# Eight linear-attention layers: keys from seven products of quarters, the queries' reciprocals through Ln and Exp, another elu, turned rows ahead

## The chip, the cores and the metric

The kernel runs on one core of a Trainium2 chip. The metric is the device time of one launch in microseconds; the figure for a kernel is the median over its runs. Five engines work at once, each through its own instructions in the order the program gives them: TensorE (PE, with its weight loads, PEld), VectorE (DVE), ScalarE (ACT), GpSimd (POOL) and SyncE (SP, which here only issues DMAs). All data are float32.

## The reference, cut to what matters

The input `x` is 512 rows of 512. Three blocks follow each other, each added to `x`: a cross-attention over 8192 context rows, eight layers of linear attention with a feed-forward part, and an expert block. The change touches the eight layers only. One layer is:

```
q = x @ Wq + bq;  k = x @ Wk + bk;  v = x @ Wv + bv
Q = elu(q) + 1;   K = elu(k) + 1
KV   = sum over the rows of K * v        # one number for each feature
Ksum = sum over the rows of K            # one number for each feature
Z = 1 / (Q * Ksum + 1e-6)
x = layernorm(x + gelu((Q * KV * Z) @ Wo + bo))
x = layernorm(x + gelu(gelu(x @ Wf1 + bf1) @ Wf2 + bf2))
```

There are no heads: keys, queries and values meet feature by feature, so `KV` and `Ksum` are vectors of 512.

## The kernel before, in words

The whole state stays on the chip. `curT` holds the rows of a layer turned (features on the partitions, 4 chunks of 128, 512 rows along the free dimension). A layer begins in `features`: twelve chunks of 128 output features (four of keys, four of queries, four of values), each the product of a 128-column piece of a weight with all of `curT`, summed over the four chunks of input features (`feature`, L628). Each float32 product shows as two instructions on PE.

The order on PE is written out by hand (`manual_schedule` for TensorE alone). The other engines' order is a planner's: it walks the program with estimated durations and gives each engine, at each point, the earliest emitted instruction that is ready by its estimate; `issue_after` keeps an instruction behind another in that order. Once fixed, every engine runs strictly in order.

At the start of a layer the last two of the four row tiles are not yet normalized: `finish` (L889 to L911) is still working on them, on DVE for the most part (gelu on ACT, residual, mean and variance, a root by Newton steps at L82, scaling at L906). So `features` first multiplies the 256 rows that exist for the first chunks, turns tile 2 (`turn`, L921: four transposes on PE, four copies with scale and shift on ACT at L923), goes on, turns tile 3, and makes up the second half, partly in pieces of one tile of 128 rows. Five PSUM banks of the pool `mm` hold the chunks under way, three of the pool `acc` serve the transposes and later sums.

Each finished piece goes to `taken`. Keys and queries pass `elu1`: two Relu and one Exp on ACT (L616, L618, L619), the sum with -1 on DVE (L620), and the final +1, on DVE with the running total for keys (L624), on ACT for queries (L622). A query chunk then gets `Q * Ksum + eps` on ACT (L977), its reciprocal on DVE (L978) and the product with Q on POOL (L979). A value chunk is multiplied with its keys and totalled on DVE (L983), and the total scales the query's row (L986):

```
nc.scalar.activation(y[ac], qf[ac], AF.Identity, bias=eps, scale=ksum[ac][:, 2:3])
nc.vector.reciprocal(y[ac], y[ac])
nc.gpsimd.tensor_tensor(y[ac], qf[ac], y[ac], ALU.mult)
```

The output projection (L1002) needs all four scaled chunks `vt[0]` to `vt[3]`. Then comes the first feed-forward product, in class `Seven`: two chunks (a pair `p`) at a time, features and rows cut into halves, so that a 2 by 2 product of quarters takes seven products instead of eight. POOL makes four sums of weight quarters for each pair (L710), DVE and POOL four sums of the turned rows (L716 to L719), PE does products 1 to 7 (L723) and DVE adds them up (L741, L759 to L779). The second feed-forward product (`SevenBack`, L839) does the same with the roles turned, first for row tiles 0 and 1, then (t = 2) for 2 and 3; in the latter call, tiles 0 and 1 are turned into the next layer's `curT` by `between`. After it, `affine` (L914, L915) makes the next layer's residual rows, for tiles 2 and 3 on POOL.

Weights come by DMA from SP's queue into the pool `big`: eight places of 1 MB, twelve weights a layer in the order wk, wq, wv, wo, four pieces of w1, four of w2. A load starts when its place is free; wk of the layer that starts at 1871.64 us is issued at 1789.84.

Of the kernel before, what the change touches and what calls it, by code (L numbers as in the profile page):

```python
# [16 lines left out]
P = 128  # L17
# [37 lines left out]
def perceiver_kernel(  # L55
# [513 lines left out]
    def layer_weights(l):  # L569
        w = [weights(big, m[l], f"{n}{l}") for m, n in ((wk, "wk"), (wq, "wq"), (wv, "wv"), (wo, "wo"))]  # L570
# [5 lines left out]
    first = layer_weights(0)  # L576
# [10 lines left out]
    def transpose_into(dst, src, t, space, tag):  # L587
# [4 lines left out]
        nc.scalar.copy(dst[:, :, t * P : (t + 1) * P], pt)  # L592

    with ExitStack() as s_:
# [10 lines left out]
        EARLY = 5  # L605

        eps = rpool.tile([P, 1], F32, name="eps")
        nc.vector.memset(eps, 1e-6)
        ncol = rpool.tile([P, C_BV - C_BQ], F32, name="ncol")
        nc.vector.tensor_scalar(ncol, col[:, C_BQ:C_BV], -1.0, None, ALU.mult)  # L610

        def elu1(ps, c, e, accum=None):

            n = ps.shape[-1]
            m = qkv.tile([P, n], F32, tag=f"m{n}", name="m")
            nc.scalar.activation(m, ps, AF.Relu, bias=ncol[:, c - C_BQ : c - C_BQ + 1], scale=-1.0)  # L616
            r = qkv.tile([P, n], F32, tag=f"r{n}", name="r")
            nc.scalar.activation(r, ps, AF.Relu, bias=col[:, c : c + 1])  # L618
            nc.scalar.activation(m, m, AF.Exp, scale=-1.0)  # L619
            nc.vector.scalar_tensor_tensor(m, m, -1.0, r, ALU.add, ALU.add)  # L620
            if accum is None:
                nc.scalar.activation(e, m, AF.Identity, bias=ones[:, 0:1])  # L622
            else:
                nc.vector.tensor_scalar(e, m, 1.0, None, ALU.add, ALU.add, accum_out=accum)  # L624
# [8 lines left out]
        def features(chunks, xT, turns, done):  # L633


            held = [(mm.tile([P, T], F32, tag="mm", name="ps"), *c) for c in chunks[:EARLY]]

            def tile_of(t, chunks_):
                for i in chunks_:
                    ps, w, c0 = held[i]  # L640
                    feature(ps, w, c0, xT, t * P, P)
                    if t % 2:
                        done(i, ps, (t - 1) * P, H)

            def half(t0, chunks_):
                for i in chunks_:
                    ps, w, c0 = held[i]
                    feature(ps, w, c0, xT, t0, H)
                    done(i, ps, t0, H)

            if 1 in turns:
                tile_of(0, (0, 1))
                turns[1]()
                tile_of(0, (2,))
                tile_of(1, (0, 1, 2))
            else:
                half(0, (0, 1, 2))
            half(0, (3,))
            if 1 in turns:
                turns[2]()  # L660
# [287 lines left out]
        for l in range(NL):  # L948
# [147 lines left out]
            def between(q):  # L1096
                if q in (2, 4):
                    turn(curT, gs[q // 2 - 1], q // 2 - 1, *c2)
# [276 lines left out]
```

## Time and profile before

| what | value |
|---|---|
| median of 3 runs | 2576.14 us (2575.96 to 2577.41) |
| the profiled execution: its own time | 2577.41 us |
| its span in the profile | 2575.6 us |
| PE, PEld, DVE, ACT, POOL busy, share of the span | 98%, 58%, 68%, 47%, 49% |
| the eight layers, from the first key product | from 1237.0 us on |
| one inner layer, start of its first key product to the next | 158.2 us (1713.41 to 1871.64) |

"Busy" is the time in which at least one instruction of an engine was in flight. Matmuls overlap, so the length of one PE record says little; the distance between the starts of records is what an instruction costs PE. The chain of work that ended last is followed back from the end of the program, at each step to what released it. All times below are microseconds from the start of the span.

### The profile page before, as it was taken

How to read it: one execution, taken by the hardware profiler on the slowest of the kernel's cores; microseconds unless marked ns; L12 is line 12 of the kernel's file. 1: busy time of each engine (PE TensorE's matmuls, PEld its weight loads, DVE VectorE, ACT ScalarE, POOL GpSimd, SP SyncE). 2: the span in 40 equal slices, each digit the busy share in tenths (PEclk: the TensorE clock that was granted, in tenths of full speed). 3: DMA queues.
4: the chain of work that ended last, by engine and by line, in shares of the span. 5: the costliest groups of instructions: out<-in, count | busy, mean ns of one | idle time of the engine just before them, and what ended most of it. 6: DMA issues, size and time to landing. Idle time of an engine off the chain costs nothing.

```text
span 2575.6 us, 32550 instructions
## 1 busy us (share of the span) xinstructions
PE 2514.4 (98%) x10984; PEld 1490.5 (58%) x10984; DVE 1747.0 (68%) x3680; ACT 1202.9 (47%) x2285; POOL 1263.1 (49%) x1422
## 2 busy tenths in 40 slices
PE   8999999999999999997999999999999999999998
PEld 4434333334343343333588686886868868687764
DVE  4466777766677776886675766757676575766764
ACT  2465666665566666663443415334153441524303
POOL 0255665666567666675054352444525354263512
PEclk9999999999999999998999999999999999999999
DMA  4111011111111111010522223222222222222236
GB/s 136 39 45 52 27 41 42 41 41 41 33 42 41 42 41 41 9 41 17 192 94 81 84 69 116 95 94 70 95 91 94 94 86 96 93 74 98 66 113 199
DMA packets 98375, 187.41 MB, mean 73 GB/s; under 512 B 10336, under 2 KB 10464, under 8 KB 98208
## 3 DMA queue, kind: packets, MB, share of 16 engines
q1 hardware_dynamic: 88496, 167.29, 20.0%
q10 hardware_dynamic: 8688, 15.94, 1.9%
q0 software_dynamic: 1024, 2.10, 0.3%
q8 instruction: 87, 1.43, 0.2%
q14 instruction: 80, 0.66, 0.1%
HBM read 162.22 MB, written 1.05 MB: 63 GB/s over the span
## 4 chain that ended last, share of the span: by engine, by line
PE 80%; DVE 9%; ACT 5%; issue 4%; POOL 2%; DMA 0%; POOLq 0%; DVEq 0%; ACTq 0%
PE pb L839 14%; PE ps L628 13%; PE pw L723 9%; PE pv L259 7%; PE po L455 7%; PE pk L230 6%; PE pc L374 6%; PE ps L723 6%; PE po L1002 4%; DVE sc L434 4%; ACT sc L377 2%; ACT sc L435 1%; POOL es L445 1%; PE pt L218 1%; PE pf L932 1%
## 5 line engine op out<-in xcount | busy, mean ns | idle before, releaser
L445 POOL TENSOR_TENSOR es<-es,sc 128x1024 f32<-128x1024 f32 x222 | 525.3, 2366 | 111.0 <-ACT sc L435 99.9
L383 DVE TENSOR_TENSOR mx<-pc,mx 128x512 f32<-128x512 f32 x448 | 283.4, 685 | 190.7 <-ACT sc L377 190.5
L435 ACT ACTIVATE sc<-sc 128x1024 f32<-128x1024 f32 x272 | 288.3, 1064 | 242.8 <-DVE sc L434 231.7
L377 ACT COPY sc<-pc 128x512 f32<-128x512 f32 x544 | 284.3, 599 | 91.4 <-PE pc L374 78.8
L434 DVE TENSOR_TENSOR sc<-sc,mbc 128x1024 f32<-128x1024 f32 x272 | 319.7, 1211 | 3.7 <-PE mbc L411 2.2
L374 PE MATMUL pc<-qT,k 64*128 64x512 f32 x1088 | 286.1, 618 | 2.9 <-ACT v L265 1.3
L455 PE MATMUL po<-sc,v 128*64 128x512 f32 x1088 | 267.5, 612 | 0.2 <-DVE mx L383 0.2
L230 PE MATMUL pk<-xn,wkv 128*128 128x512 f32 x544 | 253.2, 609 | 7.0 <-ACT v L265 2.9
L259 PE MATMUL pv<-wkv,xn 128*128 128x512 f32 x544 | 249.6, 602 | 6.3 <-DVE sin L241 3.3
L1012 ACT ACTIVATE h<-h,col 128x256 f32<-128x256 f32 x192 | 103.9, 576 | 220.8 <-DVE h L772 151.0
L374 PEld LDWEIGHTS pc<-qT,k 64*128 64x128 f32 x1088 | 100.2, 185 | 183.2 <-issue 79.8
L896 ACT ACTIVATE g<-g 128x512 f32<-128x512 f32 x64 | 39.9, 630 | 344.7 <-DVE g L856 218.7
L230 PEld LDWEIGHTS pk<-xn,wkv 128*128 128x128 f32 x544 | 99.9, 192 | 148.9 <-issue 105.9
L259 PEld LDWEIGHTS pv<-wkv,xn 128*128 128x128 f32 x544 | 98.4, 190 | 140.7 <-issue 106.7
L723 PE MATMUL pw<-curT,cur 128*128 128x256 f32 (+1 forms) x896 | 177.4, 350 | 0.1
L805 POOL TENSOR_TENSOR sh<-h 128x128 f32<-128x128 f32 x120 | 83.4, 695 | 176.3 <-PE pb L839 171.7
L979 POOL TENSOR_TENSOR y<-qf,y 128x512 f32<-128x512 f32 x32 | 44.8, 1399 | 243.6 <-DVE y L978 243.6
L723 PEld LDWEIGHTS pw<-curT,cur 128*128 128x128 f32 x896 | 150.3, 190 | 17.0 <-DVE curT L716 0.5
L856 DVE TENSOR_TENSOR g<-g,pb 128x256 f32<-128x256 f32 x135 | 50.1, 418 | 159.7 <-PE pb L839 159.2
L455 PEld LDWEIGHTS po<-sc,v 128*64 128x64 f32 x1088 | 68.3, 138 | 147.6 <-issue 124.2
L710 POOL TENSOR_TENSOR cur<-w 128x256 f32<-128x256 f32 x128 | 93.4, 740 | 118.9 <-DVE g L897 75.2
L839 PE MATMUL pb<-tw,sh 128*128 128x256 f32 x540 | 136.1, 379 | 0.0
(220 smaller groups left out, 4643.7 us busy)
## 6 DMA issues: line engine op xcount, KB each, us to landing
w<-in_wf SPq DMA_DIRECT2D x64, 1024.0 KB, 5.3
k<-cos SPq DMA_DIRECT2D x272, 64.0 KB, 2.0
cb<-in_cx SPq DMA_DIRECT2D x62, 256.0 KB, 3.4
row<-in_rows ACTq DMA_DIRECT2D x48, 256.0 KB, 4.6
f<-in_f SPq DMA_DIRECT2D x10, 1024.0 KB, 5.4
tg<-in_trig SPq DMA_DIRECT2D x16, 512.0 KB, 3.8
wk<-in_wk SPq DMA_DIRECT2D x8, 1024.0 KB, 5.2
wq<-in_wq SPq DMA_DIRECT2D x8, 1024.0 KB, 5.2
```

The source lines that it names most:

```text
L230: nc.tensor.matmul(pk, wkv[:, 0, dc, j * P : (j + 1) * P], xT[b, dc], start=(dc == 0), stop=(dc == DC - 1))
L259: nc.tensor.matmul(pv, xT[b, dc][:, t * P : (t + 1) * P], wkv[:, 1, dc, :], start=(dc == 0), stop=(dc == DC - 1))
L374: nc.tensor.matmul(pc[h], k_sb[b, p][hs, o : o + P], qT[hs, p, :], start=True, stop=True)
L377: copied[0] = nc.scalar.copy(sc[:, h, :], pc[h])
L383: behind[0] = nc.vector.tensor_tensor(mx[u][:, h, :], pc[h], mx[u][:, h, :], ALU.max)
L434: nc.vector.tensor_tensor(sc, sc, mbc[u], ALU.subtract)
L435: nc.scalar.activation(sc, sc, AF.Exp)
L445: nc.gpsimd.tensor_tensor(es[u], es[u], sc, ALU.add)
L455: nc.tensor.matmul(po[u][h * HD : (h + 1) * HD, :], v_sb[b, p][:, t * P + h * HD : t * P + (h + 1) * HD], scores[u, i][:, h, :], start=(i ...
L628: nc.tensor.matmul(ps[:, t0 : t0 + n], w[:, dc, c0 : c0 + P], xT[:, dc, t0 : t0 + n], start=(dc == 0), stop=(dc == DC - 1),)
L723: nc.tensor.matmul(ps, lhs[:, k], rhs[:, k], start=(k == 0), stop=(k == 1))
L839: nc.tensor.matmul(ps[i], lhs, rhs, start=(q == 0 and i in (1, 2, 6, 5, 4)), stop=(q == self.N - 1 and i in (1, 2, 7, 3, 4)),)
```

## The change

Keys leave `features`' list of chunks and become two pairs of the class `Seven`: `keys_of_layer` makes the sums of key-weight quarters on POOL, for layer l+1 inside the second call of `SevenBack.products` of layer l (at q = 4). For this the attention weights of l+1 are named before that call; the order of the twelve loads stays. PE begins a layer with products 1 and 2 of both pairs over the first 256 rows and the first half of two query chunks; it turns tile 2, does a third query half, turns tile 3, the second halves of the three query chunks, then products 5, 6, 7, 4 and 3 of the keys (`rest`), the fourth query chunk and the values.

The keys' ACT and DVE work on products 1 and 2 (`take`) is put behind the last normalization of the row tiles, and the queries' elu behind the copies of the turned tile 3. The two POOL affines of tiles 2 and 3 change places.

`elu1` becomes: the min side for keys on DVE instead of ACT, Exp on ACT, a new -1 on POOL, and one DVE instruction that adds 1 and the Relu side and takes the total. The queries' reciprocals wait for the fourth query chunk: four Ln on ACT, four Exp on ACT, four scale-and-shift on POOL, with small per-feature helpers. Buffers for the sums and for two query chunks come from the pool `s_h`, whose sixteen tiles hold the hidden features at other times.

```diff
-        def features(chunks, xT, turns, done):
+        def features(k7, chunks, xT, turns, done, normed):
...
+                for p in range(2):
+                    k7.p12(p, 0, H, False)
+                product(0, 0, H)
+            product(1, 0, H)
+            turns[2]()
+            with tc.issue_after(normed.ins) if normed else nullcontext():
+                for p in range(2):
+                    k7.take(p)
+            product(2, 0, H)
+            turned = turns[3]()
+            for t in range(2):
+                k7.token_sums(t)
+            with tc.issue_after(turned.ins):
+                for i in range(3):
+                    done(i, held[i], 0, H)
+            for t in (2, 3):
+                for i in range(2):
+                    product(i, t * P, P)
+            product(2, H, H)
+            with tc.issue_after(turned.ins):
+                for i in range(3):
+                    done(i, held[i], H, H)
+            k7.rest((0, 1))
+            for i in range(3, len(chunks)):
+                product(i)
+                done(i, held[i], 0, T)
...
+            def take(self, p):
+                p1, p2 = (self.held[p][:, j, :] for j in range(2))
+                o0, o1 = self.o[p] = self.tiles(p)
+                nc.scalar.copy(o1[:, :H], p1)
+                nc.vector.tensor_tensor(o0[:, :H], o1[:, :H], p2, ALU.add)
+                self.out(2 * p, o0, 0, H)
...
+            def rest(self, pairs):
+                for i in (5, 6):
+                    self.bank(*((p, i) for p in pairs))
+                    for p in pairs:
+                        (self.p5 if i == 5 else self.p6)(p)
+                self.bank(*((p, 7) for p in pairs))
+                for f in (self.add6, self.p7, self.add7, self.add5, self.p4):
+                    for p in pairs:
+                        f(p)
+                self.bank(*((p, 3) for p in pairs))
+                for f in (self.p3, self.add3):
+                    for p in pairs:
+                        f(p)
...
         def elu1(ps, c, e, accum=None):
-            nc.scalar.activation(m, ps, AF.Relu, bias=ncol[:, c - C_BQ : c - C_BQ + 1], scale=-1.0)
+            if accum is None:
+                nc.scalar.activation(m, ps, AF.Relu, bias=ncol[:, c - C_BQ : c - C_BQ + 1], scale=-1.0)
+            else:
+                nc.vector.tensor_scalar(m, ps, ncol[:, c - C_BQ : c - C_BQ + 1], 0.0, ALU.subtract, ALU.min)
             r = qkv.tile([P, n], F32, tag=f"r{n}", name="r")
             nc.scalar.activation(r, ps, AF.Relu, bias=col[:, c : c + 1])
-            nc.scalar.activation(m, m, AF.Exp, scale=-1.0)
-            nc.vector.scalar_tensor_tensor(m, m, -1.0, r, ALU.add, ALU.add)
-            if accum is None:
-                nc.scalar.activation(e, m, AF.Identity, bias=ones[:, 0:1])
-            else:
-                nc.vector.tensor_scalar(e, m, 1.0, None, ALU.add, ALU.add, accum_out=accum)
+            last = nc.scalar.activation(m, m, AF.Exp, scale=-1.0 if accum is None else 1.0)
+            nc.gpsimd.tensor_scalar(m, m, -1.0, None, ALU.add)
+            nc.vector.scalar_tensor_tensor(e, m, 1.0, r, ALU.add, ALU.add, accum_out=accum)
...
+            def weighed(e):
+                for ac in range(DC):
+                    y[ac] = fea.tile([P, T], F32, tag="y", name="y")
+                    with tc.issue_after(e.ins):
+                        e = nc.scalar.activation(y[ac], qf[ac], AF.Ln, bias=eps, scale=total[:, ac : ac + 1])
...
+                nc.vector.tensor_scalar(ks[:, 4, :], ks[:, 3, :], neps, None, ALU.mult)
+                for ac in range(DC):
+                    with tc.issue_after(e.ins):
+                        nc.scalar.activation(y[ac], y[ac], AF.Exp, scale=-1.0)
+                    nc.gpsimd.tensor_scalar(
+                        y[ac], y[ac], ks[:, 4, ac : ac + 1], ks[:, 3, ac : ac + 1], ALU.mult, ALU.add
+                    )
...
+        def keys_of_layer(w_k, xT):
+            sw = [hpool.tile([P, 2, 2, P], F32, tag="h", name="sw") for _ in range(4)]
+            k7 = Seven([(w_k, ac * P) for ac in range(DC)], xT, sw, None, None, None)
+            for p in range(2):
+                k7.weight_sums(p, (1, 2, 3, 4))
+            return k7
...
             def between(q):
                 if q in (2, 4):
                     turn(curT, gs[q // 2 - 1], q // 2 - 1, *c2)
+                if q == 4:
+                    made.append(keys_of_layer(ahead[0], curT))
...
             for t in (0, 2):
+                if t:
+                    ahead = attention_weights(l + 1)
                 g = back.products(t, row[R_BF2], between if t else lambda q: None, next_sums(t))
...
                 with tc.issue_after(last.ins):
-                    for i in range(2):
+                    for i in (1, 0) if t else (0, 1):
                         affine(cur[:, t + i, :], gs[t + i], row[R_S2], row[R_B2], nc.gpsimd if t else nc.vector)
```

`keys_taken` is what the keys' `Seven` calls with each finished half: it runs `elu1` in place and, once all four chunks are done, takes the totals' reciprocals (4 numbers a partition).

## The prediction

> **What bounds the kernel now.** First the page: who is busy, and what the chain that ended last is made of.
>
> ```profile
> PE 2514.4 (98%) x10984; PEld 1490.5 (58%) x10984; DVE 1747.0 (68%) x3680; ACT 1202.9 (47%) x2285; POOL 1263.1 (49%) x1422
> PE 80%; DVE 9%; ACT 5%; issue 4%; POOL 2%; DMA 0%; POOLq 0%; DVEq 0%; ACTq 0%
> ```
>
> That is an average over three stages, so I next asked for PE's waits in the layers alone (1230 to 2450 us), and for one inner layer as a stretch (columns: length, then busy time and count of PE, PEld, DVE, ACT, POOL, granted clock, DMA share, GB/s).
>
> ```profile
> PE pt L921 <- ACT g L910: 5.5, 8, 0.7
> PE pt L591 <- issue: 1.5, 1, 1.5
> PE ps L628 <- ACT curT L592: 0.7, 1, 0.7
> ...
> 1713.41:1871.64 158.23, 157.53 (x721) 123.24 (x720) 107.25 (x286) 60.07 (x126) 68.48 (x106) 1.00 0.27 90
> ```
>
> In an inner layer of 158.23 us PE waits once, 0.69 us, for the first turn after the projection. Nothing else holds PE: less work on PE is less time, as long as no new wait opens. DVE, ACT and POOL have room on average, so the question is room at the right places. The third view is PE's instructions of that layer in order of time (start, length, count of records).
>
> ```profile
> 1713.41 7.07 PE L628 MATMUL ps<-curT,wk 128*128 128x256 f32 x32
> 1722.48 2.25 PE L628 MATMUL ps<-curT,wk 128*128 128x128 f32 x16
> 1725.00 6.04 PE L628 MATMUL ps<-curT,wk 128*128 128x128 f32 x48
> 1742.91 13.90 PE L628 MATMUL ps<-curT,wv 128*128 128x512 f32 x32
> 1756.64 12.18 PE L1002 MATMUL po<-wo,y 128*128 128x512 f32 x28
> ```
>
> Starts give the price of a record. 256 wide: the turn after the first row starts at 1720.32, 6.91/32 = 0.216 us. 512 wide: (1756.64 - 1742.91)/32 = 0.429. 128 wide: 16 in 2.09 (the next turn starts at 1724.57) and 48 in 5.88, so 0.123 to 0.131, mean 0.127; half the columns cost more than half of 0.216.
>
> **PE, part by part.** Keys and queries with two turns take PE from 1713.41 to 1742.91 now: 29.50 us. After:
> - keys: 2 pairs x 7 products x 4 records = 56 x 0.216 = 12.10;
> - queries: three first halves and one second half, 4 x 8 x 0.216 = 6.91; two second halves in tiles of 128, 32 x 0.127 = 4.06; the fourth, 8 x 0.429 = 3.43;
> - two turns of 0.44: 0.87.
>
> Sum 27.37, so 2.13 less per inner layer, seven of them: 14.9. Layer 0 has 80 narrow records before and after; 40 x 0.216 + 24 x 0.429 = 18.9 becomes 64 x 0.216 + 8 x 0.429 = 17.3: 1.7 less. **Together 16.6 us off PE.**
>
> **A timetable for the new layer**, from its first key product (T+0), on PE: products 1 and 2 to 3.5, two query halves to 6.9, turn 2 to 7.3, third half to 9.1, turn 3 to 9.5, narrow pieces to 13.6, query half to 15.3, products 5, 6, 7, 4, 3 to 17.0, 18.7, 20.5, 22.2, 23.9, last query to 27.4, values to 41.1, projection from there. Each need is held against it.
>
> *Rows in time.* Tile 2's finish starts at T+1.0 and its scaled row is there at T+6.8, tile 3's at T+10.6 (row 1723.49 below plus 0.55). DVE works on keys between. With the keys behind the norms, the same chain at t = 0 takes 5.1 and 6.4 us (from 1689.33 to 1694.39 and 1695.75), so T+6.1 and T+7.4, against turns at 6.9 and 9.1: no wait. The copies of turn 3 on ACT (1.5 us, L923) can start at T+9.7; the pieces that read them start at 11.5. In front of them ACT may have the keys' Relu and the Exp with its table load (0.47 + 1.28 + 0.42): a wait of 0 to 1.7 us. I take 0.3 a layer, since before, ACT ran such copies 1.3 us late (transposed by 1725.0, copied from 1726.34) with no wait of PE: **2.1 us back**.
>
> *Added to the keys' path.* Fourteen DVE adds of 128x256 (0.42 each, L741 to L779: 5.8 us), six token sums on DVE (0.42 to 0.8), two on POOL (0.97, L718), two ACT copies (0.37). DVE loses four reciprocals:
>
> ```profile
> L978 DVE RECIPROCAL y<-y 128x512 f32<-128x512 f32 x20 | 66.4, 3339 | 19.6 <-ACT y L977 19.6
> L979 POOL TENSOR_TENSOR y<-qf,y 128x512 f32<-128x512 f32 x32 | 44.8, 1399 | 243.6 <-DVE y L978 243.6
> L619 ACT ACT_TABLE_LOAD x4 | 5.1, 1283 | 0.1
> L896 ACT ACT_TABLE_LOAD x5 | 6.4, 1283 | 0.1
> ```
>
> So 13.4 us leave DVE against some 9 us of adds and token sums; its elu has as many instructions for a key piece as before (Relu side moved in, the +1 merged). It ends lighter. The same adds after products 5 to 3 already run in the feed-forward part with no wait of PE; the bank for product 3 is there one that an earlier sum has freed (product 3 starts at 1789.61, before the last add of product 5 ends at 1790.08), and the last query's bank (T+23.9) can be that of a query released about T+17.
>
> *The key-weight sums.* Eight POOL sums of 0.74 (L710) = 5.9 us. POOL's last sum for the t = 2 call ends at 1705.98; eight more end at 1711.9, needed at T+15.3 = 1728.7. POOL's idle before the affines covers them; without it they cost 5.9 a layer. The key weight is loaded 80 us ahead, as its place comes free; the twelve loads keep their order on SP, and nothing is queued past them. Row loads on ACT's queue don't move.
>
> *Port.* This is where a rule speaks against the change:
>
> ```profile
> 1720.27 1.27 POOL L914 TENSOR_TENSOR cur<-g,row 128x512 f32<-128x512 f32 x1 [14.30 <-DVE g L906]
> 1720.58 0.98 DVE L82 SCALAR_TENSOR_TENSOR ny<-nt,ny 128x1 f32<-128x1 f32 x1
> 1721.81 1.23 DVE L82 SCALAR_TENSOR_TENSOR nt<-ny,vh 128x1 f32<-128x1 f32 x1
> 1723.49 0.55 DVE L906 TENSOR_SCALAR g<-g,mv,ny 128x512 f32<-128x512 f32 x1
> ```
>
> One-column instructions that take 0.15 to 0.22 elsewhere take 0.98 and 1.23 beside a POOL affine. The Trainium skill, SBUF — State Buffer, section Who interferes with whom, says why: a DVE instruction with two SBUF inputs and a POOL instruction that reads SBUF shut each other out. From T+7.4 to T+27 POOL gets four affine steps (5.4), two token sums (1.9) and the new -1, ten of 256 and two of 512 columns. No row shows POOL's one-input form at that width: at least 0.22 (L83, 4 columns), at most the two-input 0.74 and 1.40. GPSIMD Engine Reference, section Performance versus the Vector engine, has 769 ns for 512 in a good loop; I take 0.5 and 0.8: 6.6 us. DVE's two-input work there is some 8 us. Exclusive, 22 us in 20: 2 us behind; at the row's price 26 in 20: 6 us behind; without the rule nothing. What is late next is only elu, until the tail.
>
> *The tail.* The last query is done at T+27.4. ACT: two Relu and Exp to 29.2; POOL -1 to 30.1; DVE 0.63 to 30.9. ACT meanwhile: load 1.28, four Ln at the pace of L977 (0.72) to 33.4, load to 34.7, Exp 0.63 to 35.3 and each 0.57 on. POOL's four scale-and-shifts, at the dear end 1.40 each: y3 at 40.9. DVE's value total and scaling of the fourth chunk (0.1 + 0.74 + 0.08 + 0.49 after 41.1) end at 42.5; PE reads it at 41.1 + 6 x 0.429 = 43.7. Slack 1.2 behind the values; at POOL's 0.8 the values' own end decides, the same 42.5. ScalarE: Activation LUTs, section Table sets, has a set with both exp and ln, which would spare the two loads; the rows show a load at each change of function so far, Exp and Gelu, two a layer. With loads or without (2.6 us earlier), the sum is the same: hidden. Two microseconds behind on the port fit as well at 0.8; six would cost about 2 a layer. I charge **0.2 us back** in all.
>
> **Sum.** 16.6 - 2.1 - 0.2 = 14.3. The profiled execution took 2577.41 with a span of 2575.6; its span becomes 2561.3. The median of the runs is 2576.14, 1.3 under the profiled one: 2576.1 - 14.3 = **2562 us**.
>
> **The rivals.**
> - *Gain taken back* (11%): port and turn 3 together cost 2 us a layer. For it: POOL is given some 20 us of new work a layer, DVE must follow in strict order. Against: 1.2 to 4 us of slack at each need above. Time 2571 to 2581, within 0.2% (what a measurement of this kernel tells from no change).
> - *Slower* (13%): POOL's scale-and-shift with two per-partition numbers is dear. The y3 chain is 35.3 + 4 x price + 0.5, against 43.7; the 2.1 us of gain are gone from a price of (43.7 + 2.1 - 35.8)/4 = 2.5 us, twice the two-input row. At 3.0, the chain ends at 47.8, 4.1 us late: net +2.0 a layer, 2592. For it: the form isn't in the trace at this width. Against: L83, the same form, costs 0.22 at 4 columns, hardly above two-input L84 (0.20).
> - *The form gains nothing* (inside the first): 256-wide records might run slower among others. They run at 0.216 in the feed-forward part too, 224 a layer.
>
> **How the numbers follow.** Hidden but for small waits: 76%, 2556 (nearly all of 16.6, with more for narrow pieces in layer 0) to 2571. Its own range is 2556 to 2569. The 80% range takes that and the first half of the next case: 2556 to 2577. Faster by over 0.2% 0.76, within 0.11, slower 0.13.
>
> **What would show it.** Value products start 27.4 us after the first key product (29.5 before), a layer is about 155.8 to 156.4 us; PE's waits show only the 0.69 for the first turn and up to 0.7 for the copies of turn 3; the first projection follows the values at once. Wrong if PE waits for y (the tail), for DVE's token sums before product 5, or for ACT's copies by more than 1 us a layer, or if POOL's one-input rows are above 1.4 us at 512.

## The result, and the profile after

The changed kernel takes **2622.74 us** (median of four runs, 2620.88 to 2624.52) against 2576.77 in the same session: ratio 1.0177, 95% interval 1.016 to 1.0195. It is 46 us slower where 14 us less were forecast. Its profiled execution took 2622.8 us with a span of 2621.0, 45.4 above the span before.

The page of the changed kernel first, busy time by engine and the chain that ended last:

```profile
PE 2510.6 (96%) x10936; PEld 1508.8 (58%) x10936; DVE 1767.2 (67%) x3786; ACT 1199.8 (46%) x2263; POOL 1416.8 (54%) x1606
PE 76%; DVE 11%; ACT 6%; issue 4%; POOL 2%; DMA 1%; SPq 0%; DVEq 0%; POOLq 0%; ACTq 0%
```

PE is busy 4 us less in a span that is 45 us longer, and only 76% of the chain is PE's. So PE waits. Its waits in the layers (window 1230 to 2500 us; columns: total, times, longest):

```profile
PE ps L633 <- ACT r L625: 45.0, 9, 6.2
PE pt L944 <- ACT g L933: 5.5, 8, 0.7
PE pt L944 <- DVE g L929: 1.9, 7, 0.3
```

The second line is the old wait for the first turn. The first is new: nine times PE waits for ACT's Relu (L625 in `elu1`). The forecast allowed waits for rows, for token sums and for y, and has no wait for a Relu at all. One inner layer on PE, in order of time (start, length, count of records):

```profile
1889.72 3.62 PE L727 MATMUL ps<-curT,wk 128*128 128x256 f32 x16
1893.17 3.62 PE L633 MATMUL ps<-curT,wq 128*128 128x256 f32 x16
1896.62 0.60 PE L944 MATMUL pt<-ident,g 128*128 128x128 f32 x4
1897.06 1.89 PE L633 MATMUL ps<-curT,wq 128*128 128x256 f32 x8
1899.21 0.66 PE L944 MATMUL pt<-ident,g 128*128 128x128 f32 x4 [0.26 <-DVE g L929]
1906.03 7.01 PE L633 MATMUL ps<-curT,wq 128*128 128x128 f32 x40 [6.16 <-ACT r L625]
1912.88 5.34 PE L727 MATMUL pw<-sx,sw 128*128 128x256 f32 x24
1924.94 13.90 PE L633 MATMUL ps<-curT,wv 128*128 128x512 f32 x32
```

Up to turn 3 the timetable holds. Then the narrow pieces, the second halves of the first two queries, start 6.16 us late, and they go to the PSUM tiles whose first halves ACT has not read yet. What ACT does meanwhile, in the layer before (T, the first key product, is at 1725.68):

```profile
1735.48 0.51 ACT L625 ACTIVATE r<-kf,col 128x256 f32<-128x256 f32 x1 [5.78 <-DVE kf L749]
1735.90 1.49 ACT L946 ACTIVATE curT<-pt,col 128x128 f32<-128x128 f32 x4
1737.40 1.28 ACT L626 ACT_TABLE_LOAD   x1
1738.70 0.42 ACT L626 ACTIVATE m<-m 128x256 f32<-128x256 f32 x1
1739.02 0.49 ACT L625 ACTIVATE r<-kf,col 128x256 f32<-128x256 f32 x1
1739.42 0.40 ACT L626 ACTIVATE m<-m 128x256 f32<-128x256 f32 x1
1739.73 1.48 ACT L946 ACTIVATE curT<-pt,col 128x128 f32<-128x128 f32 x4
1741.10 0.48 ACT L621 ACTIVATE m<-ps,ncol 128x256 f32<-128x256 f32 x1
1741.45 0.48 ACT L625 ACTIVATE r<-ps,col 128x256 f32<-128x256 f32 x1
```

ACT stands still for 5.78 us, until DVE, busy with the norms of tiles 2 and 3, makes the keys' sum L749. Then everything comes at once and in strict order: a key's Relu, the copies of turn 2, the table load, the keys' Exp, the copies of turn 3, and only then the two Relu that read the first query's bank. They end at 1741.93; PE's narrow pieces start at 1741.99.

The wait costs more than its own length. The changed kernel by stretches (length, busy time and count of PE, PEld, DVE, ACT, POOL; then the granted clock, DMA share, GB/s):

```profile
1735.00:1738.00 3.00, 0.66 (x4) 0.42 (x4) 3.00 (x6) 2.50 (x6) 2.72 (x3) 1.00 0.00 0
1738.00:1739.00 1.00, 0.00 (x0) 0.00 (x0) 0.90 (x2) 0.99 (x2) 0.57 (x1) 0.71 0.00 0
1739.00:1742.00 3.00, 0.01 (x1) 0.01 (x1) 2.45 (x8) 3.00 (x10) 2.41 (x3) 0.50 0.00 0
1742.00:1745.00 3.00, 3.00 (x14) 3.00 (x15) 1.92 (x4) 2.42 (x7) 2.33 (x3) 0.50 0.00 0
1745.00:1746.00 1.00, 1.00 (x10) 1.00 (x10) 0.12 (x1) 0.00 (x0) 0.85 (x1) 0.88 0.36 125
```

PE's last work, turn 3, ends at 1735.84. Between 2 and 3 us after that the granted clock falls to 0.50 (0.71 on average from 1738 to 1739), and it stays there for about 3.3 us after PE has work again: the narrow pieces themselves run at half clock. The Trainium skill, TensorE: Matmul & The Clock Gate, Part 1, has a half clock after an idle window of some 3.4 us and a full one after a busy window of that length. The trace agrees in the second (3.3 us of work until the clock is back) and not quite in the first: here it fell after less idleness than a window.

**Where the 45 us are.** A layer is 164.04 us (1725.68 to 1889.72), before 158.23. Beside a kernel with the same PE order and no such wait (156.10 us a layer, run e15 below) the account is: narrow pieces begin 6.82 us after turn 3 begins instead of 0.50, so 6.32; with the third query's second half behind them they take 6.85 us instead of 5.30 until product 5, so 1.55 for the clock; together 7.87 of 7.94. The lines of e15 for it (its layer begins at 1705.84, the next at 1861.94):

```profile
1715.37 0.66 PE L960 MATMUL pt<-ident,g 128*128 128x128 f32 x4 [0.30 <-DVE g L945]
1715.87 5.47 PE L639 MATMUL ps<-curT,wq 128*128 128x128 f32 x40
1721.17 5.34 PE L742 MATMUL pw<-sx,sw 128*128 128x256 f32 x24
```

Against before: -2.13 + 7.94 = +5.81. Layers 1 to 6 are 35.4 us longer together, and the last layer, with the same wait, reaches its values 7.3 us later after its first key product. Layer 0 gives only 0.7 (waits of 1.42 and 0.47 for the same Relu) and begins 0.8 earlier. The remaining 2.8 us lie behind the last values; that stretch took 198.8 to 204.3 us in the traces here (before: 199.9; e14, below, left out), so nothing is read from them.

### The profile page after: what moved, and what is told of

It is laid out like the page before. It is cut to its first block, busy times and chain, and to the rows that moved or that the text cites. A ratio compares the mean times of both kernels' runs of the same rounds, so it can differ in the third digit from the quotient of the medians.

```text
span 2621.0 us, 32785 instructions
## 1 busy us (share of the span) xinstructions
PE 2510.6 (96%) x10936; PEld 1508.8 (58%) x10936; DVE 1767.2 (67%) x3786; ACT 1199.8 (46%) x2263; POOL 1416.8 (54%) x1606
## 4 chain that ended last, share of the span: by engine, by line
PE 76%; DVE 11%; ACT 6%; issue 4%; POOL 2%; DMA 1%; SPq 0%; DVEq 0%; POOLq 0%; ACTq 0%
PE pb L862 14%; PE pw L727 11%; PE ps L633 7%; PE pv L259 7%; PE ps L727 7%; PE pk L230 7%; PE po L455 7%; PE pc L374 6%; PE po L1070 4%; DVE sc L434 3%; ACT sc L377 2%; ACT sc L435 1%; PE pt L218 1%; PE pf L956 1%; DVE mx L383 1%
## 5 line engine op out<-in xcount | busy, mean ns | idle before, releaser
L633 PE MATMUL ps<-curT,wq 128*128 128x128 f32 (+2 forms) x584 | 130.5, 386 | 45.0 <-ACT r L625 45.0
L627 POOL TENSOR_SCALAR m<-m 128x256 f32<-128x256 f32 (+1 forms) x104 | 106.5, 1034 | 117.3 <-ACT m L626 115.1
L633 PEld LDWEIGHTS ps<-curT,wq 128*128 128x128 f32 x584 | 101.0, 220 | 64.6 <-ACT r L625 47.1
```

What stands on the lines that cost most here:

```text
L633: nc.tensor.matmul(ps[:, t0 : t0 + n], w[:, dc, c0 : c0 + P], xT[:, dc, t0 : t0 + n], start=(dc == 0), stop=(dc == DC - 1),)
```

## Experiments

The theory: PE waits because the second half of a query shares a PSUM tile with a first half that ACT reads late, and ACT reads it late because of the order of the program. Rivals: the new arithmetic is too much work for ACT, DVE and POOL in the first 14 us of a layer, whatever its order; or one of its parts (logarithms, POOL's -1) is the cause.

**1. The tile.** First the reads early. In the changed kernel the first halves of queries 0 and 1 go to `elu1` ahead of turn 2:

```diff
             product(1, 0, H)
+            for i in range(2):
+                done(i, held[i], 0, H)
             turns[2]()
...
-                for i in range(3):
+                for i in range(2, 3):
                     done(i, held[i], 0, H)
```

> The new kernel, with the elu of the first halves of query chunks 0 and 1 emitted ahead of turn 2 instead of behind turn 3; nothing else changed. Theory A (a bank is the unit of waiting: the second half of a query chunk is written into the PSUM bank whose first half ACT has not read yet, so PE waits for that reading; and turn 3's copies are late as a second cause): PE's wait of 6.2 us a layer for ACT's Relu goes, and what is left is a wait of about 2 us for turn 3's copies, which still stand behind the keys' Exp on ACT; a layer falls by some 4 to 5 us, the run by 30 to 36 us to 2587 to 2592. Rival B (the port between DVE and POOL, or POOL's new work, holds the rows of the queries): the wait only moves, the run stays within 8 us of 2622.

Run e1: 2617.89 us, 1.0158 of the kernel before (1.0138 to 1.0179): a miss in size. The wait for L625 is gone, as the theory says, but 4.6 us a layer at the copies of turn 3 take its place (32.3 us in 14 waits, two of them 3.25 and 1.33 us in one layer):

```profile
PE ps L633 <- ACT curT L948: 32.3, 14, 3.3
```

The other way round, ACT is left as it is and the second halves of queries 0 and 1 get a PSUM tile of their own:

```diff
+            own = acc.tile([P, 2, H], F32, tag="acc", name="own")
             for t in (2, 3):
                 for i in range(2):
-                    product(i, t * P, P)
+                    w, c0 = chunks[i]
+                    for dc in range(DC):
+                        nc.tensor.matmul(
+                            own[:, i, (t - 2) * P : (t - 1) * P], w[:, dc, c0 : c0 + P],
+                            xT[:, dc, t * P : (t + 1) * P], start=(dc == 0), stop=(dc == DC - 1),
+                        )
```

> The new kernel, all ACT and DVE work in its place, but the second halves of query chunks 0 and 1 go into a PSUM bank of their own. Theory A: PE no longer waits for ACT's Relu on the first halves; the pieces of tile 2 run at once, those of tile 3 wait for turn 3's copies, about 3.5 us instead of 6.4, and the third chunk, whose halves still share a bank, may wait 1 to 2 us for its Relu; a layer falls by 2 to 4 us, the run to 2594 to 2608. If the wait is not one of banks, nothing changes: within 4 us of 2622.

Run e6: 2614.09 us, 1.0143 (1.0123 to 1.0164), again a miss in size. The narrow pieces of queries 0 and 1 no longer wait for a Relu but for rows; the wait for the Relu moves to query 2, which still shares its tile:

```profile
PE ps L633 <- ACT r L625: 17.5, 8, 2.3
PE own L678 <- ACT curT L959: 13.7, 14, 1.4
```

The tile is confirmed as the place of the wait, and the 6 us shrink to 3.9 a layer; but behind it the next need is late too. Third, the old kernel, where nothing but the elu of the first halves of two key chunks, and with it the reading of their PSUM tiles, is put behind turn 2's copies:

```diff
-                turns[2]()
+                turned = turns[2]()
+                with tc.issue_after(turned.ins):
+                    for i in (0, 1):
+                        done(i, held[i][0], 0, H)
```

> The kernel before, with one thing moved: in the layers after the first, the elu of the first halves of chunks 0 and 1 (keys) is emitted behind the copies of turn 2 instead of at once; PE's order is the same. Theory A (bank): PE, which writes tile 2 of the same two chunks into the same banks, now waits for ACT's Relu: about 1.7 us for chunk 0 and 0.3 to 1 for chunk 1, so 2 to 3 us a layer and 14 to 20 us in all: 2590 to 2597. If it is not the bank, the time stays within 4 us of 2577.

Run e5: 2594.31 us, 1.0067 (1.0046 to 1.0087), as expected. With none of the new arithmetic the old kernel has the same wait:

```profile
PE ps L628 <- ACT r L618: 15.0, 13, 1.9
```

**2. The order.** The changed kernel without its priority for turned rows: `take` and the queries' elu are emitted behind their products, with no `issue_after`.

```diff
             product(1, 0, H)
+            for i in range(2):
+                done(i, held[i], 0, H)
             turns[2]()
-            with tc.issue_after(normed.ins) if normed else nullcontext():
-                for p in range(2):
-                    k7.take(p)
```

(`take` moves up behind products 1 and 2, the third first half's elu behind its product.)

> The new kernel without its priority for the turned rows: the keys' work on products 1 and 2 and the elu of query chunks 0 and 1 are emitted ahead of turn 2, that of chunk 2 ahead of turn 3, with nothing put behind the last norm or the copies. Theory A: ACT works during PE's first 9 us again, PE does not wait for ACT's Relu; what is left is DVE's finish of tiles 2 and 3, slowed by the keys' work as before (turn 3 about 1.5 to 3 us late). A layer 157.5 to 159.5 us, the run 2570 to 2590. Rival B (POOL's and the port's new work is the cause wherever it stands): above 2600.

Run e7: 2594.35 us, 1.0067 (1.0047 to 1.0087), a little above the expected span. No Relu wait of weight is left. PE waits 2.17 us a layer for tile 3's row, because DVE now works on keys between the norms (two of their sums, with a POOL affine beside them, take 1.51 and 1.48 us):

```profile
PE pt L943 <- DVE g L928: 15.2, 7, 2.2
```

So the priority costs 28 of the 46 us, and what it was there for, the rows, is worth 2.2 us of wait a layer. Its opposite, the keys' `take` put later still, behind the copies of turn 3:

```diff
-            with tc.issue_after(normed.ins) if normed else nullcontext():
+            with tc.issue_after(turned.ins):
                 for p in range(2):
                     k7.take(p)
```

(and moved behind turn 3 in the program.)

> The new kernel, with the keys' ACT and DVE work on products 1 and 2 put behind the copies of turn 3 instead of behind the last norm; the queries' elu stays where it is. Theory A: turn 3's copies come some 2 us earlier, but the keys' Relu and Exp with the table load still stand ahead of the queries' Relu on ACT; the wait stays about the same or falls by up to 2 us, a layer 0 to 2 us less: 2608 to 2622. Theory A2 (the late copies of turn 3 alone are the cause): the wait of 6.2 us a layer falls below 2: below 2590.

Run e2: 2658.61 us, 1.0316 (1.0296 to 1.0337): a clear miss. I had expected ACT to be free earlier. Instead it did nothing for 9.74 us, in the last 3.9 of them with turn 2's rows ready in PSUM:

```profile
1750.55 0.33 ACTq L986 DMA_DIRECT2D row<-in_rows  x1
1750.93 1.15 ACT L946 ACTIVATE curT<-pt,col 128x128 f32<-128x128 f32 x3 [9.74 <-POOL cur L937]
```

The load of the next rows is issued from ACT's queue; its place is released by POOL's affine step, and the planner had now put it ahead of the copies. Both moves together (e1 and e2):

> Both: the elu of the first halves of query chunks 0 and 1 ahead of turn 2, and the keys' ACT and DVE work behind the copies of turn 3. Theory A: no wait of PE for ACT above 0.7 us a layer; a layer is 156 to 157 us, the run 2562 to 2570, which is what the prediction had for the change itself. Rival B: still above 2600.

Run e3: 2636.81 us, 1.0228 (1.0211 to 1.0245), a miss again. The second halves of queries 0 and 1 run at once; that of query 2 waits for its own first half:

```profile
PE ps L633 <- ACT r L625: 56.3, 8, 7.8
```

In the trace POOL's four affine steps fill 1741.64 to 1747.78, ahead of its -1 for queries 0 and 1; DVE, in order, waits for that -1 and so makes the keys' sum only at 1753.02; ACT's queue stands behind it. So, in addition, the affine steps of tiles 2 and 3 behind the -1 of the queries' second halves (`less_one` is that instruction, `later` is `rows_on` of the layer before):

```diff
+            with tc.issue_after(less_one[0].ins):
+                later()
             k7.rest((0, 1))
...
+            def rows_on(cur=cur, gs=gs, row=row):
+                for t in (2, 3):
+                    affine(cur[:, t, :], gs[t], row[R_S2], row[R_B2], nc.gpsimd)
```

> The kernel of e3_both, with one more thing moved: the four POOL steps of the affines of tiles 2 and 3 come behind the -1 of the queries' second halves on POOL instead of ahead of every -1. If POOL's order is what held ACT in e3_both (DVE stood 3.6 us for a -1 queued behind the affines, the keys' adds behind it, ACT's Relu of the keys behind those, the third query's Relu behind that), PE's wait of 7.5 us a layer falls to 3 to 4.5 and the run from 2637 to 2605 to 2615; also DVE's Newton steps run at 0.2 us and turn 3 no longer waits for its rows. If POOL's order does not matter, the wait stays above 6.5.

Run e12: 2614.16 us, 1.0144 (1.0123 to 1.0164), as expected. Turn 3 no longer waits for its row (DVE's one-column steps are not slowed), and query 2's wait falls from 7.8 to 4.1 us. From here the reads were ordered by their need: query 0 ahead of turn 2's copies, query 1 behind them, query 2 behind turn 3's, the keys' `take` last, with buffers of their own for the three (the affines stay where e12 put them):

```diff
+            done(0, held[0], 0, H, normed)
+            turned = turns[2]()
+            with tc.issue_after(turned.ins):
+                done(1, held[1], 0, H, normed)
             product(2, 0, H)
             turned = turns[3]()
             with tc.issue_after(turned.ins):
+                done(2, held[2], 0, H, normed)
                 for p in range(2):
                     k7.take(p)
```

> The new kernel in another order, all parts of it kept: the first query chunk's Relu and Exp on ACT ahead of turn 2's copies, the second's right behind them, the third's right behind turn 3's, the keys' work on products 1 and 2 behind that; the sum on DVE of these three pieces behind the last norm, with their Relu and Exp results in tiles of their own; POOL's affines of tiles 2 and 3 behind the second halves' -1. Theory A: no wait of PE above 1 us; a layer 156 to 157.3 us, the run 2560 to 2572: the gain that the prediction had. Rival B: above 2590.

Run e8: 2595.69 us, 1.0073 (1.0056 to 1.009): a miss. Turns and all narrow pieces now run without a wait, and the next need in line is late, product 5:

```profile
1736.46 7.13 PE L734 MATMUL pw<-sx,sw 128*128 128x256 f32 x24 [2.80 <-DVE sx L727]
```

DVE's token sums stand behind its sums of the three query pieces, which wait for POOL. These 24 records take 7.13 us; undisturbed they take 5.34: the clock again (0.74 and 0.50 in the two stretches of 2 us after 1736). One more step puts the token sums right behind the norms, and behind them `take`'s DVE sums and those of the three query pieces (`late`):

```diff
+            with tc.issue_after(normed.ins) if normed else nullcontext():
+                for t in range(2):
+                    summed = k7.token_sums(t)
             with tc.issue_after(turned.ins):
                 for p in range(2):
-                    k7.take(p)
+                    k7.take(p, summed)
+            with tc.issue_after(summed.ins):
+                for f in late:
+                    f()
```

> The reordered kernel, with VectorE's token sums put right behind the norms, and its sums of the three early query pieces and its additions for the keys' first two products behind those token sums. Theory (program order alone made TensorE wait; the arithmetic saved is real): no wait of TensorE above 1 us in a layer, so no stretch with a granted clock near 0.50; a layer of 156.0 to 157.5 us against 158.2 in the kernel before, and a run of 2556 to 2572 us. Rival (the new form has too much work on ScalarE, VectorE and POOL in the first 14 us, so that a wait only moves on): another wait of 2 to 4 us a layer, at the projection for y or in the keys' sums, and a run of 2585 to 2600 us.

Run e9: 2580.95 us, 1.0012 (1.0003 to 1.0022), between the two expectations: the rival's kind of wait, smaller than it said. Of the changed kernel's loss 42 us are undone by the order of the work and buffers for three query pieces, with no arithmetic changed, and PE's clock doesn't fall. Values start 27.56 us after the first key product (forecast 27.4), with one wait of 0.37 us for a key sum in it. But the layer is 158.81 us, since y comes late:

```profile
1747.98 0.69 ACT L624 ACTIVATE m<-ps,ncol 128x512 f32<-128x512 f32 x1 [0.87 <-DVE kf L634]
1749.78 1.28 ACT L1034 ACT_TABLE_LOAD   x1
1751.08 2.93 ACT L1034 ACTIVATE y<-qf,eps,ks 128x512 f32<-128x512 f32 x4
1754.02 1.28 ACT L1044 ACT_TABLE_LOAD   x1
1756.85 0.49 DVE L1068 TENSOR_SCALAR y<-y,kvs 128x512 f32<-128x512 f32 x1 [3.75 <-POOL y L1045]
1757.39 1.12 PE L1086 MATMUL po<-wo,y 128*128 128x512 f32 x2 [0.82 <-DVE y L1068]
```

The last query's product ends at about 1742.7; its Relu runs at 1747.98. ACT has the Relu and Exp of the last key pieces in front of it, which DVE's min side lets begin only at 1743.33 and which last to 1747.11; then it waits 0.87 us until DVE's sum of a key piece frees the buffer. From there the chain of y takes 9.4 us. The projection, from the end of the values to the feed-forward part, takes 17.6 us against 15.1 before.

**3. The parts.** The logarithms alone, in the old kernel:

```diff
-                        nc.scalar.activation(y[ac], qf[ac], AF.Identity, bias=eps, scale=ksum[ac][:, 2:3])
-                        nc.vector.reciprocal(y[ac], y[ac])
-                        nc.gpsimd.tensor_tensor(y[ac], qf[ac], y[ac], ALU.mult)
+                    if ac == DC - 1:
+                        for a in range(DC):
+                            y[a] = fea.tile([P, T], F32, tag="y", name="y")
+                            with tc.issue_after(e.ins):
+                                e = nc.scalar.activation(y[a], qf[a], AF.Ln, bias=eps, scale=ksum[a][:, 2:3])
+                        for a in range(DC):
+                            with tc.issue_after(e.ins):
+                                nc.scalar.activation(y[a], y[a], AF.Exp, scale=-1.0)
+                            nc.gpsimd.tensor_tensor(y[a], qf[a], y[a], ALU.mult)
```

> The kernel before with one part of the change alone: the queries' reciprocals as exponentials of logarithms on ScalarE (four logarithms, four exponentials, then the four products on POOL), in place of Identity, VectorE's reciprocal and POOL's product; keys, elu and the order of turns are the old ones. If this part costs nothing, as predicted (VectorE has it easier, ScalarE's two table loads and eight passes lie beside TensorE's values): within 4 us of the kernel before, with no new wait of TensorE. If it is one of the causes: a wait of TensorE ahead of the projection or in the next stage of 0.5 us a layer or more, and 2581 us or more.

Run e13: 2578.4 us, 1.0004 (0.9995 to 1.0013), no new wait, a layer of 158.20: hidden, as expected, two more table loads a layer and all. And the reverse, e9 with the old reciprocals on DVE, in the place of the logarithms:

```diff
-                        e = nc.scalar.activation(y[ac], qf[ac], AF.Ln, bias=eps, scale=total[:, ac : ac + 1])
...
-                        nc.scalar.activation(y[ac], y[ac], AF.Exp, scale=-1.0)
-                    nc.gpsimd.tensor_scalar(
-                        y[ac], y[ac], ks[:, 4, ac : ac + 1], ks[:, 3, ac : ac + 1], ALU.mult, ALU.add
-                    )
+                    nc.scalar.activation(y[ac], qf[ac], AF.Identity, bias=eps, scale=total[:, ac : ac + 1])
+                    nc.vector.reciprocal(y[ac], y[ac])
+                    nc.gpsimd.tensor_tensor(y[ac], qf[ac], y[ac], ALU.mult)
```

> The kernel with the token sums first, but with the queries' reciprocals as they were before (Identity on ScalarE, reciprocal on VectorE, product on POOL). If the logarithms are needed with the new keys, because the last query comes 14 us before the projection and VectorE is full there: TensorE waits 3 to 6 us a layer for y and loses 1 to 2 us more to the lower clock, 30 to 55 us more than the kernel with the token sums first. If it makes no difference where y is made: within 5 us of it.

Run e14: 2662.01 us, 1.0327 (1.0312 to 1.0343), 81 us above e9, where 30 to 55 were expected. With seven products the keys' totals are complete only when the last query is; four reciprocals follow each other then, and the fourth product on POOL ends 10 us after the values:

```profile
1780.90 12.98 DVE L1034 RECIPROCAL y<-y 128x512 f32<-128x512 f32 x4
1794.02 1.26 POOL L1035 TENSOR_TENSOR y<-qf,y 128x512 f32<-128x512 f32 x1 [1.95 <-DVE y L1034]
...
PE po L1074 <- DVE y L1056: 77.1, 8, 10.4
```

Logarithms cost nothing where they weren't needed, and in this order the new keys need them. Next POOL's -1, left out in the changed kernel (e17) and in e9 (e15):

```diff
-            nc.gpsimd.tensor_scalar(m, m, -1.0, None, ALU.add)
-            nc.vector.scalar_tensor_tensor(e, m, 1.0, r, ALU.add, ALU.add, accum_out=accum)
+            nc.vector.scalar_tensor_tensor(e, m, 0.0, r, ALU.add, ALU.add, accum_out=accum)
```

(These two kernels leave out the pair of -1 and +1, which is more than rounding: by the arithmetic, the pair turns the tiny Exp of a far negative query into an exact zero before the division. They measure time only.) In e15 one thing more changes. `less_one`, behind which POOL's affines come, is then ACT's Exp:

```diff
-            less_one[0] = nc.gpsimd.tensor_scalar(m, m, -1.0, None, ALU.add)
+            less_one[0] = last
```

> The changed kernel in its own order, without POOL's step of -1 in the elu and nothing else changed. If POOL's step is itself what makes ScalarE read the banks late, most of the loss goes: 2560 to 2585 us. If it is the order of the instructions, TensorE's wait for ScalarE's Relu stays at 5 to 6 us a layer: 2605 to 2623 us.

Run e17: 2621.09 us, 1.0171 (1.0154 to 1.0188): nothing gained, the wait for L625 stays at 44.6 us. POOL's step had no share in the first wait.

> The kernel with the token sums first, without POOL's step of -1 in the elu: VectorE adds the exponential and the Relu part directly (exp - 1 + 1 is left out as a pair, so the function is the same up to rounding). Theory (the gain is lost at the projection, where y comes about 2.5 us late, because each elu piece passes through POOL between ScalarE and VectorE and holds its buffers the longer): no wait of TensorE for y or for the keys' sums, a layer of 156.0 to 157.0 us, a run of 2558 to 2568 us. Rival (y is late by the chain of two table loads, four logarithms and four exponentials alone): y still about 2 us late, 2574 to 2581 us.

Run e15: 2562.18 us, 0.9941 (0.9926 to 0.9956), in the middle of what was expected: no wait for y, values 27.39 us after the first key product, a layer of 156.10. The run brings the forecast time, but it doesn't single out POOL's step, because the affines moved with it. The first of them, in e9 (a layer from 1715.12 on) and in e15 (from 1705.84 on):

```profile
1737.66 2.74 POOL L953 TENSOR_TENSOR cur<-g,row 128x512 f32<-128x512 f32 x2
1711.88 1.30 POOL L953 TENSOR_TENSOR cur<-g,row 128x512 f32<-128x512 f32 x1 [12.82 <-DVE g L945]
```

So POOL's four affines run from T+22.5 to T+27.9 in e9, beside DVE's last work on the keys, and from T+6.0 to T+12.3 in e15. How much of the gain is theirs and how much is the step's, no run tells.

**4. A kernel with all of the work.** e9 with POOL's step beside the exponential: the Relu side first, POOL adds 1 to it while ACT makes the other side, DVE adds the two with -1.

```diff
             nc.scalar.activation(r, ps, AF.Relu, bias=col[:, c : c + 1])
+            less_one[0] = nc.gpsimd.tensor_scalar(r, r, 1.0, None, ALU.add)
...
-            less_one[0] = nc.gpsimd.tensor_scalar(m, m, -1.0, None, ALU.add)
-                nc.vector.scalar_tensor_tensor(e, m, 1.0, r, ALU.add, ALU.add, accum_out=accum)
+                nc.vector.scalar_tensor_tensor(e, m, -1.0, r, ALU.add, ALU.add, accum_out=accum)
```

> The kernel with the token sums first, with POOL's one-input step put beside ScalarE's exponential in place of behind it: the Relu part comes first and POOL adds 1 to it while ScalarE makes the other part and its exponential; VectorE then adds (exp - 1) and (Relu + 1). All the work of the reference is done. Theory (what cost the kernel with the token sums first its gain was POOL's step as a link of the chain ScalarE, POOL, VectorE): no wait of TensorE for y, a layer of 156.2 to 157.2 us, a run of 2560 to 2569 us. Rival (POOL's twelve steps cost time wherever they stand, since they and VectorE's two-input work hold each other up): y late again by 1 us or more, 2572 to 2582 us.

Run e18: 2573.85 us, 0.9986 (0.9977 to 0.9995). The time lies in the rival's span. It is 0.1% faster than the kernel before, but PE still waits for y (0.42 and 0.38 us in one layer) and a layer is 157.79. The affines, behind the +1 that comes earlier now, begin at T+20.2 instead of T+22.5, so part of the 7 us against e9 may be theirs. The rival has its part: beside POOL's affine steps DVE takes 1.51 us for a sum of 0.42. So, last, those affine steps behind the last query's step, where POOL has 6 us with nothing to do:

```diff
-            with tc.issue_after(less_one[0].ins):
-                later()
             k7.rest((0, 1))
             for i in range(3, len(chunks)):
                 product(i)
                 done(i, held[i], 0, T)
+                if i == 3:
+                    with tc.issue_after(less_one[0].ins):
+                        later()
```

> The kernel with POOL's step beside the exponential, and with POOL's four affine steps for the next residual (128x512, two inputs) put behind the last query's step, where POOL waits some 6 us for ScalarE's logarithms. Theory (what is left of the delay of y are VectorE's two-input instructions between T+18 and T+23, 1.51 and 1.72 us long beside POOL's affine steps): y early enough, no wait of TensorE for it, a layer of 156.2 to 157 us, a run of 2560 to 2568 us. Rival (the affine steps only trade places with another delay, POOL's scale-and-shift of y now behind them): y late by 0.5 us or more, 2570 to 2580 us.

Run e19: **2559.9 us**, 0.9937 (0.9923 to 0.995) of the kernel before, at the lower end of what was expected: faster than both kernels, with all of the work done. PE's waits in the layers are the old ones and one of 0.3 us in the whole run, and the projection follows the values at once:

```profile
PE ps L743 <- ACT midT L963: 0.3, 1, 0.3
...
1707.21 3.62 PE L743 MATMUL ps<-curT,wk 128*128 128x256 f32 x16
1734.14 13.90 PE L639 MATMUL ps<-curT,wv 128*128 128x512 f32 x32
1747.87 12.18 PE L1087 MATMUL po<-wo,y 128*128 128x512 f32 x28
1862.86 3.62 PE L743 MATMUL ps<-curT,wk 128*128 128x256 f32 x16
```

A layer is 155.65 us, values begin 26.93 us after the first key product.

## Why the prediction was wrong

- *PE, part by part*: right, and a little too careful. 27.37 us to the values were worked out; e19, with no wait on the way, shows 26.93 (e9 and e15 each have a short wait in their 27.56 and 27.39). The 0.44 are the narrow pieces: 0.113 us a record in e19 where 0.127 was taken. 16.6 us off PE were forecast, and e19 is 16.5 below the kernel before. That the two are so close is partly luck: by the last values its profiled execution has taken 19.4 us less for the layers, and behind them it loses 4.1, within the spread of that stretch.
- *A timetable for the new layer*: **the step that failed.** It checked each PE step for its inputs, and the place of its output only for product 3 and the last query. "Narrow pieces to 13.6" needs ACT's reading of the first query's PSUM tile by T+9.5; ACT had done it at T+16.25. The term missing from the sum is 6.32 us a layer. Together with the clock, which I left at 1.00 throughout, 7.9 us a layer against a gain of 2.13. The old kernel has the same need and meets it: in the layer from 1713.41 on, ACT has read the first chunk by 1716.2, and PE writes on into its tile at 1722.48. e5 shows that PE waits as soon as that reading is put back.

```profile
1715.71 0.47 ACT L618 ACTIVATE r<-ps,col 128x256 f32<-128x256 f32 x1
```

- *Rows in time*: right for tile 2's row, there at T+5.96 (forecast 6.1); wrong for tile 3's, at T+9.45 (7.4), and for the copies. The model for the rows was the chain at t = 0, where POOL has no affine step; here POOL starts one as soon as tile 2's row is ready, and DVE's one-column steps take 1.19 and 1.31 us beside it, as in the rows that the prediction itself shows under *Port*. That cost only 0.26 us. The copies of turn 3 were to start at T+9.7 or at most 1.7 later; they started at T+14.05. I listed what ACT "may have" in front of them one piece at a time, and not as a queue that opens all at once when DVE comes to the keys.
- *Added to the keys' path*: "it ends lighter" is wrong. In a layer DVE is busy 110.69 us against 107.25, although the logarithms alone bring it to 94.83 (e13). Part of that is work beside POOL: two key pieces' min side took 2.29 us at 1735.70, beside POOL's affines, and 0.60 in e9, where POOL stood still. Even in e19 DVE is busy 107.36 us a layer, as much as before.
- *The key-weight sums*: no run shows a wait for them; hidden, as forecast.
- *Port*: the sort of loss was right ("what is late next is only elu, until the tail"), the size not. POOL's -1 takes 0.90 and 1.49 us where 0.5 and 0.8 were estimated, above the 1.4 named under "Wrong if". In the changed kernel that costs nothing (e17). What it costs once the first wait is gone isn't singled out: e15 is 18.8 us faster than e9, but with the affines in another place; and e19, which keeps the step, is no slower than e15.

```profile
L627 POOL TENSOR_SCALAR m<-m 128x256 f32<-128x256 f32 x80 | 71.3, 897 | 58.3 <-ACT m L626 56.2 <-DMA wv<-in_wv 1.3
L627 POOL TENSOR_SCALAR m<-m 128x512 f32<-128x512 f32 x24 | 35.5, 1490 | 59.0 <-ACT m L626 58.9
L1029 POOL TENSOR_SCALAR y<-y,ks 128x512 f32<-128x512 f32 x32 | 27.5, 872 | 38.6 <-ACT y L1028 33.0 <-DVE ks L1025 5.6
```

- *The tail*: the scale-and-shift is 0.87 (0.8 taken), and in the changed kernel nothing waits for y. But that kernel reaches its values 7.8 us later than forecast. Near the forecast speed (e9) the last Relu came 5 us after its product, not at once, because the last key pieces stood in front of it on ACT and held its buffers; the projection is 2.5 us a layer longer, where 0.2 in all were charged.
- *Rivals*: the slower one, a dear scale-and-shift, did not happen. None named the wait that decided. *Gain taken back* has the time of e9, not of the changed kernel, and names the port and turn 3, where e9 waits for y.

## What to carry to other kernels

When an engine's steps are moved or grouped, write down for each matmul not only when its operands are there but who must have read its output's PSUM tile first; where two halves of a tile are written at different times, the reader of the first half is on the path of the second. A priority for the work that seems urgent holds up everything behind it on a strictly ordered engine, and the first wait hides the next ones: here the needs (PSUM tile, rows, token sums, y) were late behind each other, and each repair showed the next. A step handed from engine to engine is priced by the queue it stands in on each of them: moving POOL's four affine steps to where POOL waits, and nothing else, was worth 14 us here (e18 to e19).

## What the runs showed of the hardware that I had not expected

- A PE wait of 2.8 us was enough to bring the granted clock to 0.50 (e8), and the work after it ran 1.8 us longer; after 6.2 us it was 1.55 us. In e7, with a wait of 2.17 and one of 0.33 behind it, the next 40 records took some 6.9 us instead of 5.5 (e15). So in these three kernels a wait of 2 to 6 us cost 1.4 to 1.8 us on top of itself. The prediction has no term for it, since before the clock was 1.00 in the layers.
- POOL's one-input add of a constant took 1.49 us at 128x512, its scale-and-shift with two numbers for each partition, on the same shape, 0.87. The instruction with more to do was the cheaper one. Why, was not tried.
- A DMA issue on ACT's queue, waiting for a place that POOL releases, held back ACT's copies of rows that had been ready for 3.9 us (e2).
- Whether the wait between two halves of a PSUM tile is the program's own, which keeps its books by tile, or would be needed on the chip as well, was not tried.
